# Cross-attention scores: two 64-row tiles of TensorE for four 32-row tiles, with a rest of 16 rows per head

## The chip, the cores and the metric

The kernel runs on one core of a Trainium2 chip. The metric is the device time of one launch in microseconds, as the median of several runs. A profiled execution of the same program gives the trace that the prediction reads. Names of engines: PE is TensorE's matmul, PEld its weight load, DVE VectorE, ACT ScalarE, POOL GpSimd, SP SyncE.

## The reference

There are 16 sequences in a batch, with 100 queries of 640 features, 8 heads of 80 features, and 718 context keys of 384 features (the last 4 of 722 context rows feed a second, small attention). Everything is float32.

```python
query = hidden_states @ Wq            # 100 x 640
keyt = enc @ Wk                       # 718 x 640
valt = enc @ Wv
hs = _mha(query, keyt, valt)          # scores, softmax, weighted values for 8 heads of 80
...                                   # a second attention of x with itself and with 4 tokens: ca_hs2
out = (hs + ca_hs2) @ Wout + b_out + residual
```

What the change touches is the first product in `_mha`: for each sequence, head and key, the dot product of 80 features of the query with 80 features of the key.

## The kernel before

**Tiling.** A loop over the 16 sequences (`for b in range(B)`) does for each of them: scores, the maximum over keys (DVE), the second attention (POOL above all), the next sequence's keys and values (`kk`, `vv`, lines L471 and L440), exponentials (ACT), the weighted values (`a_ps`, L1317), and on some turns the queries of the next two sequences (L541) and the output projection (L951). Inside the loop the order of instructions on every engine is the order in which the Python code issues them (`tc.manual_schedule`); ahead of the loop a scheduler orders them.

**Scores.** Keys lie transposed, `kT[partition, c, u, key]`, in five chunks `c` of 128 partitions; queries likewise in `qp` (chunks 0 to 3, one sequence of 100 columns at a time) and `qz` (chunk 4). The 718 keys are split into six blocks of 119 or 120. A call `scores(b, g, tiles)` makes the scores of two of these blocks (`a` = 0, 1) for all eight heads, so there are three calls for a sequence, one behind the other. Its output has keys on partitions (120) and queries of two heads, 200 columns, side by side in each of four PSUM banks `s_ps[r]`. A head has 80 features: 64 of them lie in chunks 0 to 3 and 16 in chunk 4.

Before the change TensorE is used as four row tiles of 32 rows. Row tile `r` holds the heads 2r and 2r+1: chunk 0 and 1 are the two 32-row halves of the first head's 64 features, chunks 2 and 3 those of the second head, and chunk 4 has 16 rows of each of the two heads. For chunk 4 the queries are in `qz` twice, once masked to the first head's 16 rows and once to the second head's, so one matmul with 200 moving columns serves both heads. The loop order is: block `a`, chunk `c`, row tile `r`. Each matmul names its own stationary 120 key columns. An f32 matmul appears in the trace as two weight loads and two matmul records (two passes).

**Banks.** Calls 0 and 2 take two double banks of pool `ps2`, call 1 takes two banks of `psk` and two of `ps1`. ACT copies finished banks to SBUF (L631, L637). Behind the third call TensorE turns to `now.softmax2()` (L808, output in column tiles of 32) and `second.products()` (L746, the whole array).

**Set-up.** The layout of the features comes from `load_packed`, which loads `Wk` transposed into the chunks by nine DMAs (L305), and from the copies of `Wq` on DVE (L1070 and L1077). Both run once, ahead of the loop.

The functions that the diff touches, with the lines of the profile:

Of the kernel before, what the change touches and what calls it, by code (L numbers as in the profile page):

```python
# [14 lines left out]
B, S, H = 16, 100, 640  # L15
NH, D = 8, 80
CAD, T = 384, 4
SK = 722 - T
P = 128
HC = H // P  # L20
# [3 lines left out]
KN = KT // 2  # L24
# [26 lines left out]
for h in range(NH):  # L51
    lo = h * D
    while lo < (h + 1) * D:
        c = lo // P
        hi = min((h + 1) * D, (c + 1) * P)
        PIECES.append((h, c, lo - h * D, lo - c * P, hi - lo))
        lo = hi
# [15 lines left out]
RG = 4  # L73


def load_packed(load, to, w):

    rows = w.rearrange("(r u k) n -> r u k n", r=RG, u=2)
    for r, u in [(r, u) for r in range(RG) for u in range(2)]:
        load(  # L80
            out=to[32 * r : 32 * r + 32, 2 * u : 2 * u + 2],
            in_=rows[r, u, :64].rearrange("(j p) n -> p j n", j=2),
        )
    load(out=to[:, 4], in_=w.rearrange("(h k) n -> h k n", h=NH)[:, 64:])


# [46 lines left out]
def kernel(  # L133
# [18 lines left out]
    nc = tc.nc  # L152
# [14 lines left out]
    def pair(name):  # L167
        tile = ps2.tile([P, 2, 512], F32, tag="ps2", name=name)
        return tile
# [21 lines left out]
    def scores_tile(name):  # L191
        return main.tile([P, 2, ROWS], F32, tag="st", name=name, bufs=NP)
# [13 lines left out]
    def vb_tile(name):  # L206
        return main.tile([P, T, H], F32, tag="vb", name=name)
# [16 lines left out]
    def load_enc(b):  # L224
        enc = enc_tile(f"enc_{b}"), None
        for u, lo, hi in ((0, 0, 3), (1, 1, 3), (2, 0, 2)):
            at = A_RAW[u, lo]
            nc.sync.dma_start(
                out=enc[0][:, at : at + hi - lo],
                in_=enct[b][:, lo:hi, u * (KT - 1) : u * (KT - 1) + KT],  # L230
            )
        return enc

    def load_rest(b, enc):
        if b == 1:
            room = hsT_tile("rest_1").rearrange("p c s -> p (c s)")
            rest = room[:, : len(A_REST) * KT].rearrange("p (i k) -> p i k", k=KT)
        else:
            rest = rest_tile(f"rest_{b}")
        for (u, c), i in A_REST.items():  # L240
            nc.sync.dma_start(
                out=rest[:, i], in_=enct[b][:, c, u * (KT - 1) : u * (KT - 1) + KT]
            )
        return enc[0], rest
# [6 lines left out]
    def a_form(enc, f):  # L251
        return enc[0][:, A_AT[f]]
# [8 lines left out]
    wq_sb = const.tile([P, HC, H], F32, name="wq_sb")  # L261
    kT = const.tile([P, HC, 3, KT], F32, name="kT")
# [20 lines left out]
    for g in range(2):  # L283
        for c in range(CC):
            nc.scalar.dma_start(
                out=wv_sb[:, 2 * c + g],
                in_=wv[c * P : (c + 1) * P, g * (H // 2) : (g + 1) * (H // 2)],
# [14 lines left out]
    ca_0 = small.tile([S, T, S], F32, tag="ca", name="ca_0", bufs=2)  # L302
    in_order(nc.sync.dma_start(out=ca_0, in_=cas[0].unsqueeze(0).to_broadcast([S, T, S])))
    load_packed(
        lambda **ends: in_order(nc.sync.dma_start(**ends)), wkt_sb[:, :, :CAD], wkt  # L305
    )
    halves = [t[:, u] for t in [scores_tile(f"wq_{i}") for i in range(NP)] for u in range(2)]
    room = halves.pop()
    wq_in = [t[:, :H] for t in halves]
# [19 lines left out]
    for h, c, r, s, k in PIECES:  # L329
        nc.gpsimd.dma_start(  # L330
            out=m2[s : s + k, c, GROUPS[c][1].index(-1), h * T : (h + 1) * T],
            in_=wqcat[h * D + r : h * D + r + k, :],
# [4 lines left out]
    for c in range(HC):  # L337
        first = c * P - HEADS[c][0] * D
        nc.gpsimd.affine_select(
            out=hmask[:, c], in_=hmask[:, c], compare_op=ALU.is_ge, fill=0.0,  # L340
# [3 lines left out]
            out=hmask[:, c], in_=hmask[:, c], compare_op=ALU.is_ge, fill=0.0,  # L344
# [71 lines left out]
    class Values(Blocks):  # L416
# [17 lines left out]
        def product(self, at, f, first, last):  # L434
            for bank in "AB":
                if self.opened[bank] is at and bank in self.fresh:
                    first = True
                    self.fresh.discard(bank)
            for j in range(2):
                nc.tensor.matmul(  # L440
                    at[0][j][:KN, : H // 2],
                    a_form(self.enc, f)[:, j * KN : (j + 1) * KN],
                    wv_there.get(f, wv_sb[:, W_AT[f]]),
                    start=first,
                    stop=last,
                    skip_group_check=True,
                )
# [152 lines left out]
    def scores(b, g, tiles):  # L600

        qp, qz = tiles
        name = f"s_ps_{b}_{g}"
        if g == 1:
            s_ps = [f(f"{name}_{r}") for r, f in enumerate((psumk, psumk, psum1, psum1))]
        else:
            pairs = [pair(f"{name}_{i}") for i in range(2)]
            s_ps = [pairs[r // 2][:, r % 2] for r in range(RG)]
        n = KN
        for a in range(2):  # L610
            u, j = KC[2 * g + a]
            for c in range(HC):
                for r in range(RG):
                    rows = slice(32 * r, 32 * r + 32)
                    if c < 4:
                        rhs = qp[rows, c // 2, c % 2, (b % 2) * S : (b % 2 + 1) * S]
                        lo, hi = (c // 2) * S, (c // 2 + 1) * S
                    else:
                        rhs, lo, hi = qz[rows, 0, b % 2], 0, 2 * S
                    nc.tensor.matmul(  # L620
                        s_ps[r][:n, 256 * a + lo : 256 * a + hi],
                        kT[rows, c, u, j * KN : (j + 1) * KN],
                        rhs,
                        start=(a == 0 and c == 0),
                        stop=(c == HC - 1),
                        skip_group_check=True,
                    )
        st = scores_tile(f"st_{b}_{g}")[:n]
        if g == 1:
            for r in range(RG):  # L630
                nc.scalar.copy(  # L631
                    st[:, :, 2 * r * S : 2 * (r + 1) * S],
                    s_ps[r][:n].rearrange("p (a q) -> p a q", a=2)[:, :, : 2 * S],
                )
        else:
            for i in range(2):
                nc.scalar.copy(  # L637
                    st[:, :, 4 * i * S : 4 * (i + 1) * S].rearrange(
                        "p a (r q) -> p r a q", r=2
                    ),  # L640
                    pairs[i][:n].rearrange("p r (a q) -> p r a q", a=2)[:, :, :, : 2 * S],
                )
        return st
# [81 lines left out]
    class Second:  # L725
# [98 lines left out]
        def load(self):  # L824
            b = self.b
            self.vb = vb = vb_tile(f"vb_{b}")
            nc.gpsimd.dma_start(
                out=vb[:S],
                in_=va_d[b * T : (b + 1) * T, :].unsqueeze(0).to_broadcast([S, T, H]),
            )  # L830
# [179 lines left out]
    for n in range(HC):  # L1010
        for c in range(CC):
            for lo in (0, 64):
# [4 lines left out]
                    start=(c == 0),  # L1017
                    stop=(c == CC - 1),
# [14 lines left out]
    for c in range(HC):  # L1033
        m_ps = psum(f"m_ps_{c}")
        for n, heads in enumerate(HEADS):
# [4 lines left out]
                start=(n == 0),  # L1040
                stop=(n == HC - 1),
                skip_group_check=True,
# [23 lines left out]

    with tc.issue_after(summed.ins):
        for c in range(HC):
            for u in range(2):
                nc.vector.tensor_copy(  # L1070
                    wq_sb[:, c, 2 * u * P : 2 * (u + 1) * P].rearrange(
                        "p (a r k) -> p a r k", a=2, r=RG
                    ),
                    wq_in[c].rearrange("p (r k) -> p r k", r=RG)[:, :, u * D : u * D + 64]
                    .rearrange("p r (a k) -> p a r k", a=2),
                )
            nc.vector.tensor_copy(  # L1077
                wq_sb[:, c, 4 * P :].rearrange("p (h k) -> p h k", h=NH),
                wq_in[c].rearrange("p (h k) -> p h k", h=NH)[:, :, 64:],
            )  # L1080
# [7 lines left out]
    for c in range(CC):  # L1088
        for n in range(2):
# [4 lines left out]
                start=(c == 0),  # L1094
                stop=(c == CC - 1),
# [3 lines left out]
    for n in range(2):  # L1099
        nc.scalar.dma_start(  # L1100
            out=va_d[:, n * (H // 2) : (n + 1) * (H // 2)],
            in_=va[n * B * T : (n + 1) * B * T],
# [10 lines left out]
    last, enc_next, second_next = None, load_rest(1, load_enc(1)), Second(1, xT)  # L1113
# [8 lines left out]
    for b in range(B):  # L1122
        p = b // 2
# [37 lines left out]
        if b == 0:  # L1161
            enc_sums(enc)
            now.load()
            now.softmax1()
        st.append(scores(b, 0, tiles))
        if b == 0:
            now.exponentials1()
        nc.vector.tensor_tensor(most[:KN], st[0][:, 0], st[0][:, 1], ALU.max)
        st.append(scores(b, 1, tiles))
        larger(1)  # L1170
        st.append(scores(b, 2, tiles))

        now.softmax2()
# [131 lines left out]
        for g in range(2):  # L1305
# [6 lines left out]
            for h, i in order:  # L1312
# [3 lines left out]
                for lo, hi in QC:  # L1316
# [4 lines left out]
                        start=(i == 0 and h in (0, *range(4, NH))),  # L1321
                        stop=(i == len(KC) - 1),
                        skip_group_check=True,
# [16 lines left out]
        last = mine  # L1340
# [55 lines left out]
```

## Time and profile before

| | |
|---|---|
| Time, median of 3 runs | 943.8 us (943.6 to 943.82) |
| Span of the profiled execution | 942.4 us, 1.4 us less than the median of the runs |
| PE busy | 934.5 us (99% of the span) |
| PEld busy | 796.2 us (84%) |
| DVE / ACT / POOL busy | 674.0 / 364.7 / 623.1 us |
| Granted TensorE clock | 1.000 over the span |
| `s_ps` matmuls (L620) on the chain that ended last | 12% of the span |

How to read it: the span runs from the first to the last instruction of the profiled execution. Busy time is the union of an engine's records. The duration of a matmul record contains the time that it waits in the array for its weights and a fixed tail, so it is longer than the distance between the starts of consecutive matmuls; rates are read from those distances. Single starts and durations that are named in the prediction and that no shown line contains are those of the same trace, one record at a time.

### The profile page before, as it was taken

The numbers are of one execution on the slowest core, as the hardware profiler recorded it, in microseconds if no ns is written. First come the engines' busy times: TensorE is split into PE (matmuls) and PEld (weight loads), VectorE is DVE, ScalarE is ACT, GpSimd is POOL, SyncE is SP. The second block draws the span as 40 slices with busy tenths as digits, with TensorE's granted clock in tenths as the row PEclk, the third lists the DMA queues.
The fourth block names the chain that finished last, engine by engine and source line by source line (L and its number), as shares of the span: only waits on it lengthen the run. The fifth ranks groups of instructions, "written<-read, shape, count | busy, mean of one in ns | idle before, by whom it ended". The sixth has DMA issues, their size and how long they took to land.

```text
span 942.4 us, 25629 instructions
## 1 busy us (share of the span) xinstructions
PE 934.5 (99%) x11215; PEld 796.2 (84%) x11215; DVE 674.0 (72%) x1084; ACT 364.7 (39%) x605; POOL 623.1 (66%) x565
## 2 busy tenths in 40 slices
PE   9999999999999999999999999999999999999998
PEld 6998979888797888989789887987989888897866
DVE  3559794977929688595955959578693886949684
ACT  1244443524334244433424334244431534334241
POOL 5857976776738757495873948657694576748514
PEclk9999999999999999999999999999999999999999
DMA  8822024040310404003050130403113030210300
GB/s 264 296 60 87 3 70 128 1 130 3 94 60 1 117 2 135 5 11 122 1 151 3 37 82 1 139 1 95 38 40 113 1 112 7 59 53 1 95 8 29
DMA packets 45367, 62.48 MB, mean 66 GB/s; under 512 B 13448, under 2 KB 37320, under 8 KB 43656
## 3 DMA queue, kind: packets, MB, share of 16 engines
q1 hardware_dynamic: 41720, 42.97, 15.2%
q0 software_dynamic: 2512, 16.72, 6.1%
q8 instruction: 88, 1.44, 0.6%
q10 hardware_dynamic: 1024, 1.15, 0.4%
q14 instruction: 23, 0.19, 0.1%
HBM read 55.26 MB, written 5.57 MB: 65 GB/s over the span
## 4 chain that ended last, share of the span: by engine, by line
PE 96%; DVE 3%; issue 0%; DMA 0%; ACT 0%; POOL 0%; ACTq 0%; DVEq 0%
PE s_ps L620 12%; PE a_ps L1317 12%; PE v_psA L440 10%; PE v_psB L440 8%; PE kT_ps L565 8%; PE k_psA L471 7%; PE q_ps L541 7%; PE o_ps L951 7%; PE k_psB L471 6%; PE v_psC L440 3%; PE k_psC L471 3%; PE y_ps L746 2%; PE v_ps L381 2%; PE v_psD L440 2%; PE v_psE L440 2%; PE k_psE L471 1%
## 5 line engine op out<-in xcount | busy, mean ns | idle before, releaser
L781 POOL TENSOR_TENSOR e<-ca,g 100x800 f32<-100x800 f32 x64 | 99.8, 1570 | 145.2 <-DVE most L1156 125.0
L870 POOL TENSOR_TENSOR hs<-vb,p 100x640 f32<-100x640 f32 x64 | 105.6, 1659 | 45.9 <-DVE p L856 32.5
L877 POOL TENSOR_TENSOR hs<-hs,hs 100x640 f32<-100x640 f32 x48 | 113.9, 2373 | 3.8
L1317 PEld LDWEIGHTS a_ps<-vs,st 120*36 120x36 f32 (+3 forms) x3072 | 109.1, 125 | 5.6 <-issue 5.5
L1317 PE MATMUL a_ps<-vs,st 120*36 120x81 f32 (+3 forms) x3072 | 111.9, 233 | 0.0
L440 PE MATMUL v_psA<-wv_sb,enc 128*120 128x320 f32 x352 | 109.5, 434 | 0.0
L506 POOL TENSOR_TENSOR enc<-enc 128x240 f32<-128x240 f32 x135 | 98.1, 736 | 16.9 <-DMA enc<-in_enct 9.8
L1144 DVE TENSOR_TENSOR st<-st,over 120x1600 f32<-120x1600 f32 x48 | 107.6, 2243 | 0.0
L637 ACT COPY st<-s_ps 120x800 f32<-120x800 f32 x64 | 49.7, 829 | 135.6 <-PE s_ps L620 135.6
L620 PE MATMUL s_ps<-qp,kT 32*120 32x100 f32 x3072 | 97.4, 263 | 0.0
L620 PEld LDWEIGHTS s_ps<-qp,kT 32*120 32x120 f32 x3072 | 94.7, 179 | 1.6 <-issue 0.2
L788 POOL TENSOR_TENSOR e<-e,e 100x800 f32<-100x800 f32 x48 | 90.4, 1884 | 3.8
L440 PE MATMUL v_psB<-wv_sb,enc 128*120 128x320 f32 x296 | 91.9, 433 | 0.0
L471 PE MATMUL k_psA<-enc,wk_sb 128*128 128x240 f32 x360 | 87.6, 366 | 0.0
L1329 DVE RECIPROCAL rs<-a_ps 100x4 f32<-100x4 f32 x32 | 5.8, 182 | 111.0 <-PE a_ps L1317 111.0
L1156 DVE TENSOR_TENSOR most<-most,st 120x800 f32<-120x800 f32 x64 | 66.2, 1034 | 24.1 <-ACT st L631 23.0
L1152 ACT ACTIVATE st<-st 120x1600 f32<-120x1600 f32 x48 | 73.9, 1539 | 22.3 <-DVE st L1144 22.2
L471 PEld LDWEIGHTS k_psA<-enc,wk_sb 128*128 128x128 f32 x360 | 68.2, 190 | 16.8 <-DVE kT L411 0.2
L440 PEld LDWEIGHTS v_psA<-wv_sb,enc 128*120 128x120 f32 x352 | 63.2, 183 | 22.6 <-issue 0.5
L471 PE MATMUL k_psB<-enc,wk_sb 128*128 128x240 f32 x300 | 73.1, 366 | 0.3 <-DVE sm L853 0.3
L440 PEld LDWEIGHTS v_psB<-wv_sb,enc 128*120 128x120 f32 x296 | 54.0, 183 | 21.9 <-DVE vs L411 0.4
L541 PE MATMUL q_ps<-xT,wq_sb 128*128 128x200 f32 x400 | 69.1, 333 | 0.0
(146 smaller groups left out, 1732.8 us busy)
## 6 DMA issues: line engine op xcount, KB each, us to landing
vb<-va_d POOLq DMA_DIRECT2D x16, 1000.0 KB, 7.4
enc<-in_enct SPq DMA_DIRECT2D x30, 240.0 KB, 3.9
enc<-in_enct SPq DMA_DIRECT2D x15, 360.0 KB, 3.6
xT<-in_xt SPq DMA_DIRECT2D x8, 500.0 KB, 4.3
rest<-in_enct SPq DMA_DIRECT2D x31, 120.0 KB, 6.6
xn<-in_x SPq DMA_DIRECT2D x11, 320.0 KB, 5.7
out<-xn SPq DMA_DIRECT2D x11, 320.0 KB, 3.2
ca<-in_cas SPq DMA_DIRECT2D x16, 156.2 KB
```

The source lines that it names most:

```text
L440: nc.tensor.matmul(at[0][j][:KN, : H // 2], a_form(self.enc, f)[:, j * KN : (j + 1) * KN], wv_there.get(f, wv_sb[:, W_AT[f]]), start=first ...
L471: nc.tensor.matmul(at[:, i * KT : (i + 1) * KT], wk_sb[:, W_AT[f], i], a_form(self.enc, f), start=(first and i == 0), stop=last, skip_grou ...
L506: nc.gpsimd.tensor_tensor(out, left, right, op)
L541: nc.tensor.matmul(q_ps[:, : 2 * S].rearrange("p (j s) -> p j s", j=2), wq_sb[:, c, n * P : (n + 1) * P], xT[:, :, c, :], start=(c == 0), ...
L565: nc.tensor.matmul(bank[:, i * KT : (i + 1) * KT], weights[c], a_raw(enc, u, c), start=(i == 0 and c == 0), stop=(c == CC - 1), skip_group ...
L620: nc.tensor.matmul(s_ps[r][:n, 256 * a + lo : 256 * a + hi], kT[rows, c, u, j * KN : (j + 1) * KN], rhs, start=(a == 0 and c == 0), stop=( ...
L781: first = nc.gpsimd.tensor_tensor(to, self.ca[:, t, :].unsqueeze(1).to_broadcast([S, NH, S]), g[:, :, t].unsqueeze(2).to_broadcast([S, NH, ...
L788: nc.gpsimd.tensor_tensor(e, e, to, ALU.add)
L870: first = nc.gpsimd.tensor_tensor(to, vb[:S, t, :].rearrange("p (h d) -> p h d", h=NH), p2[:, :, t].unsqueeze(2).to_broadcast([S, NH, D]), ...
L877: nc.gpsimd.tensor_tensor(sums, sums, to, ALU.add)
L1144: return nc.vector.tensor_tensor(st[i], st[i], top.over[:KN].unsqueeze(1).to_broadcast([KN, 2, ROWS]), ALU.subtract,)
L1317: nc.tensor.matmul(a_v[lo:hi, h % 4], st[i // 2][: KEYS[i], i % 2, h * S + lo : h * S + hi], block(i, h // 4)[: KEYS[i], h % 4], start=(i ...
```

## The change

The 64 leading features of a head are contracted in one 64-row tile of TensorE where two 32-row passes were accumulated. Chunk `c` of 0 to 3 now holds the head `c` on partitions 0 to 63 and the head `4 + c` on partitions 64 to 127, so two matmuls of 64 rows and 100 columns stand for four of 32 rows. The rest of 16 rows per head stays as it was: four matmuls of 32 rows with the masked `qz` and 200 columns. In a call all 64-row matmuls of both blocks now stand together, and so do all 32-row matmuls; calls 0 and 2 begin with the 64-row kind, call 1 with the 32-row kind. Weight set-up follows the new layout: eight DMAs of 64 partitions for eight of 32 partitions with the same bytes, and five wide DVE copies for ten. TensorE has 3622 instruction rows in its program for 3878; no other instruction of it moves, and the order on the other engines is the same.

```diff
 def load_packed(load, to, w):
-    rows = w.rearrange("(r u k) n -> r u k n", r=RG, u=2)
-    for r, u in [(r, u) for r in range(RG) for u in range(2)]:
-        load(
-            out=to[32 * r : 32 * r + 32, 2 * u : 2 * u + 2],
-            in_=rows[r, u, :64].rearrange("(j p) n -> p j n", j=2),
-        )
+    rows = w.rearrange("(h k) n -> h k n", h=NH)
+    for half in range(2):
+        for c in range(4):
+            load(
+                out=to[64 * half : 64 * half + 64, c],
+                in_=rows[4 * half + c, :64],
+            )
     load(out=to[:, 4], in_=w.rearrange("(h k) n -> h k n", h=NH)[:, 64:])
...
         n = KN
-        for a in range(2):
+        opened = set()
+
+        def product(a, c, rows, bank, lo, rhs, last):
             u, j = KC[2 * g + a]
-            for c in range(HC):
+            nc.tensor.matmul(
+                s_ps[bank][:n, 256 * a + lo : 256 * a + lo + rhs.shape[-1]],
+                kT[rows, c, u, j * KN : (j + 1) * KN],
+                rhs,
+                start=bank not in opened,
+                stop=last,
+                skip_group_check=True,
+            )
+            opened.add(bank)
+
+        def halves(last):
+            for a in range(2):
+                for c in range(HC - 1):
+                    for half in range(2):
+                        rows = slice(64 * half, 64 * half + 64)
+                        rhs = qp[rows, c // 2, c % 2, (b % 2) * S : (b % 2 + 1) * S]
+                        product(a, c, rows, 2 * half + c // 2, c % 2 * S, rhs, last)
+
+        def rests(last):
+            for a in range(2):
                 for r in range(RG):
                     rows = slice(32 * r, 32 * r + 32)
-                    if c < 4:
-                        rhs = qp[rows, c // 2, c % 2, (b % 2) * S : (b % 2 + 1) * S]
-                        lo, hi = (c // 2) * S, (c // 2 + 1) * S
-                    else:
-                        rhs, lo, hi = qz[rows, 0, b % 2], 0, 2 * S
-                    nc.tensor.matmul(
-                        s_ps[r][:n, 256 * a + lo : 256 * a + hi],
-                        kT[rows, c, u, j * KN : (j + 1) * KN],
-                        rhs,
-                        start=(a == 0 and c == 0),
-                        stop=(c == HC - 1),
-                        skip_group_check=True,
-                    )
+                    product(a, HC - 1, rows, r, 0, qz[rows, 0, b % 2], last)
+
+        for part, last in zip((rests, halves) if g == 1 else (halves, rests), (False, True)):
+            part(last)
...
-            for u in range(2):
-                nc.vector.tensor_copy(
-                    wq_sb[:, c, 2 * u * P : 2 * (u + 1) * P].rearrange(
-                        "p (a r k) -> p a r k", a=2, r=RG
-                    ),
-                    wq_in[c].rearrange("p (r k) -> p r k", r=RG)[:, :, u * D : u * D + 64]
-                    .rearrange("p r (a k) -> p a r k", a=2),
-                )
+            nc.vector.tensor_copy(
+                wq_sb[:, c, : 4 * P].rearrange("p (n i k) -> p i n k", n=4, i=2),
+                wq_in[c].rearrange("p (i n k) -> p i n k", i=2, n=4)[:, :, :, :64],
+            )
```

## The prediction

> **What bounds the kernel.** First the page: how busy each engine is, then the chain of work that ended last.
>
> ```profile
> PE 934.5 (99%) x11215; PEld 796.2 (84%) x11215; DVE 674.0 (72%) x1084; ACT 364.7 (39%) x605; POOL 623.1 (66%) x565
> PEclk9999999999999999999999999999999999999999
> PE 96%; DVE 3%; issue 0%; DMA 0%; ACT 0%; POOL 0%; ACTq 0%; DVEq 0%
> ```
>
> TensorE is the bound, at full clock. Its list of waits holds 1.2 us on DVE in the loop and next to nothing else. So each nanosecond that TensorE needs more or less in the scores reaches the end; nothing is there to absorb it or to take its place.
>
> Next, the timeline of TensorE over one sequence's scores (start us, length us, group, count):
>
> ```profile
> 273.32 0.53 PE L1317 MATMUL a_ps<-vs,st 119*36 119x81 f32 x10
> 273.78 1.10 PE L620 MATMUL s_ps<-qp,kT 32*120 32x100 f32 x32
> 274.69 0.54 PE L620 MATMUL s_ps<-qz,kT 32*120 32x200 f32 x8
> 275.05 1.00 PE L620 MATMUL s_ps<-qp,kT 32*120 32x100 f32 x32
> 275.87 0.54 PE L620 MATMUL s_ps<-qz,kT 32*120 32x200 f32 x8
> ...
> 280.59 0.54 PE L620 MATMUL s_ps<-qz,kT 32*120 32x200 f32 x8
> 281.05 0.75 PE L808 MATMUL z_ps<-y,e 100*32 100x33 f32 x64
> ```
>
> The scores take 281.05 - 273.78 = 7.27 us per sequence, 116 us in all. A block of keys is 32 records of 100 columns (8 rounds: 4 chunks x 2 passes, four tiles side by side) in 0.82 us, then 2 rounds of 200 columns in 0.36 us.
>
> Third, the durations by line (min/median/max ns), which show what a round waits for:
>
> ```profile
> L620 PE MATMUL s_ps<-qp,kT x3072: 244/263/342, 59.8 to 898.6; 32*120 32x100 f32 x192
> L620 PE MATMUL s_ps<-qz,kT x768: 327/338/413, 60.7 to 898.9; 32*120 32x200 f32 x192
> L746 PE MATMUL y_ps<-m,xT x160: 244/260/327, 27.6 to 847.0; 128*100 128x96 f32 x96, 128*100 128x128 f32 x64
> L541 PE MATMUL q_ps<-xT,wq_sb x400: 332/332/437, 51.1 to 830.9; 128*128 128x200 f32 x134
> ```
>
> The 100-column matmul has three durations. 244 (5 rounds per sequence) is the pure one: its weights were loaded under the 200-column round ahead of it, and the next round starts 86 ns later. 263 (42 rounds) is 19 longer: it waits for weights, and rounds are 105 ns apart. 342 (1 round, the first behind `a_ps`) waits 98: its load began only when the tile shape had changed. The 200-column rounds last 347 and 327 by turns, waits of 20 and 0, starts 188 and 169 apart.
>
> **Why 105.** Distances between loads that a next load holds up, read one by one: 58 ns for `k2_ps` (64 columns, two column tiles), 88 for `y_ps` (100 columns, all 128 rows), 112 for `m_ps` (128 columns, all rows), 105 here (120 columns, four 32-row tiles). All four are columns x 0.83 + 5 ns. Neither the number of rows nor the number of tiles enters. One row stands outside: the f32 transposes load 128 columns every 85 ns, but their load records last 142 ns for 190 and the change has none.
>
> **What the change removes.** Half of the 100-column matmuls: 1536 records of 3072. But the rounds stay: 4 chunks x 2 passes per block, now two tiles of 64 rows side by side for four of 32. Each streams 100 columns (86) and loads 120 (105). Two tiles fewer per round start 6.6 ns apart, which the 105 hides. No row has 64-row tiles; from both sides: 32 rows give 105 and 128 rows lie on the same line, so I take 105. If the load were free, the floor is 86.
>
> The Trainium skill prices side-by-side tiles otherwise ("TensorE: Matmul & The Clock Gate", section "The mechanism", and "Measured speedup vs the span model"): the span is one matmul plus about 4 ns for each further tile. By that, two tiles fewer save 8 ns in 48 x 16 rounds, an estimate of 6 us, and the sum below would be 946 us. The trace has no such term where a load bounds the round, so it is not used.
>
> **What it adds: changes of tile shape.** Before, the three calls of a sequence are 32-row work from first to last. After, the order is 64 | 32, 32 | 64, 64 | 32: three more changes per sequence. What a change costs, in two terms:
> - A gap. Distance from the last start of one shape to the first of the next, less the undisturbed distance: 162 - 70 from `a_ps` to `s_ps` (above: last start 273.32 + 0.53 - 0.23 = 273.62, next 273.78), 262 - 169 from `q_ps` to `a_ps`, 362 - 269 from `o_ps` to `a_ps`, 179 - 86 from the transposes to `a_ps`, 257 - 169 from `s_ps` to `z_ps`. That is 88 to 93 whatever the two shapes; I take 93.
> - Weights that are not loaded ahead: 98 here, 437 - 332 = 105 for `q_ps`, 327 - 246 = 81 for `y_ps`: again the load of one tile.
>
> No row has a change between two row heights. The Trainium skill ("TensorEngine Tiling (Array Packing)", "Key Properties") says that a change of tiling mode, not of the tile alone, drains the engine, and lists 64-row and 32-row tiling as different modes; no run here shows that pair, and the sum needs only the rows above. Bounds: zero (32-row tiles inside the 64-row ones need no change) and 93 + 98. Every pair seen costs the upper, so I take it.
>
> **The sum per sequence**, in ns. Streams are the same on both sides: 48 x 86 + 12 x 169 = 6156, and the exit to `z_ps` costs 88 on both.
> - Before: waits 98 + 42 x 19 + 6 x 20 = 1016. Total 6156 + 1016 + 88 = 7260, against 7270 measured.
> - After, 48 rounds of 64 rows: two are first behind a change (98 each), 46 wait 19: 1070. The old rounds without a wait are gone, since no 200-column round stands ahead of them. 12 rounds of 32 rows: two first ones at 98, the others hide their load (105) under the stream (169): 196. Gaps 3 x 93 = 279. Total 6156 + 1070 + 196 + 279 + 88 = 7789.
>
> That is +529 per sequence, +8.5 us over 16. On the profiled execution 942.4 + 8.5 = 950.9; on the median of the runs, which is 1.4 above that span, 952.3.
>
> **Other edits, all at nothing.** The DVE copies (L1070, ten of 284 ns) end at 32.5 us and the queries need them at 51.2; without that cover, five wider copies in place of ten still cost no more. The eight DMAs of `load_packed` carry the same bytes and rows, and stand at the same place of SP's queue (issued from 11.8 to 23.5 us, the `Wq` loads behind them); `w_ps` needs the first of them at 28.2 us, then for chunk 0 the fifth in place of the seventh, and up to 29.1 us the chain waits for POOL's `m2` anyway, so some 0.9 us of cover; without it a late one would cost its lateness once. In call 1 banks 0 and 2 finish some rounds earlier, so ACT's copy may start earlier; it is no bound (39%). In calls 0 and 2 the banks finish together at the end as before, and ACT's two copies of 829 ns fit under the next call's 2.4 us. In the first sequence `qz` comes 66 ns late for its first round (a record of 413); it is needed later now. TensorE's first matmul of call 1 waits for banks that `a_ps` had, as before. All that stands behind the scores moves by the same amount, so no new wait.
>
> **The rivals.**
> - *Half price.* The gap of 93 is paid, but weights are prefetched across a change of row height: waits become 98 + 46 x 19 + 2 x 20 = 1012, +275 per sequence, +4.4 us, 948.2. Against it: every first round behind a change in this trace waits. For it: none of those is between two row heights.
> - *No change of shape.* 32-row and 64-row tiles follow each other like tiles of one kind: 1012 for 1016, 943.7, no change. Against it: five other pairs all pay.
> - *Faster: tiles share the load port.* If 105 were four loads taking turns at 26 ns, two would hide under the stream and 64-row rounds would be 86 apart. Then waits are 2 x 98 + 196 = 392, with gaps 671 for 1016: -345 per sequence, -5.5 us, 938.3. It decides as soon as a 64-row round waits less than 19 - 529/46 = 7.5 ns, that is comes every 93 or less. Against it: one tile of 100 columns takes 88, two of 64 take 58; four in turn would not lie on that line.
> - *Much slower.* Two 64-row loads do not overlap each other: a round of 210, +105 x 46 x 16 = +77 us. Against it: two and four tiles overlap here, with starts 6.6 ns apart.
>
> **How the numbers follow.** Full price 0.68 (952.3), half price 0.14 (948.2), no change of shape 0.09, shared port 0.05, loads in turn 0.04. A measurement here tells about 0.2% (1.9 us) from no change, so slower is 0.68 + 0.14 + 0.04 = 0.86, the same 0.09, faster 0.05. The range takes the first two cases with some room: 946.0 to 955.5.
>
> **What the profile after would show.** 64-row matmuls, 1536 records, most of 263 ns with rounds 105 apart, 64 records of about 342. 32-row matmuls of 200 columns mostly 327, 128 of about 425. A sequence's scores 7.8 us long, and `s_ps` at 13% of the chain. I am wrong if 64-row rounds come under 93 ns apart, if the start behind a change of row height is under 150 ns (100 columns) or 220 ns (200 columns) later, or if the first round behind it does not last longer.

## The result: 951.83 us for 943.81, and the profile after

The changed kernel takes 951.83 us (median of 4 runs, 951.51 to 951.97) beside 943.81 us for the kernel before in the same comparison: a ratio of 1.0084, 95% interval 1.007 to 1.0098. It is slower by 8.0 us. The forecast was 952.3 us, with a range of 946.0 to 955.5. The profiled execution has a span of 950.1 us, 7.7 more than before.

The page after, on the engines and the chain:

```profile
PE 943.5 (99%) x9679; PEld 798.3 (84%) x9679; DVE 681.0 (72%) x1079; ACT 364.6 (38%) x605; POOL 620.7 (65%) x565
PE 96%; DVE 2%; DMA 1%; issue 0%; ACT 0%; POOL 0%; ACTq 0%; DVEq 0%
```

TensorE has 1536 matmul records fewer (768 matmuls of two records each) and is 9.0 us longer busy. It still carries 96% of the chain.

The timeline of TensorE over the scores of the same sequence as before (start us, length us, group, count):

```profile
274.27 0.60 PE L1326 MATMUL a_ps<-vs,st 119*36 119x81 f32 x12
274.80 1.93 PE L615 MATMUL s_ps<-qp,kT 64*120 64x100 f32 x32
276.65 1.63 PE L615 MATMUL s_ps<-qz,kT 32*120 32x200 f32 x32
278.21 3.60 PE L615 MATMUL s_ps<-qp,kT 64*120 64x100 f32 x64
281.75 0.95 PE L615 MATMUL s_ps<-qz,kT 32*120 32x200 f32 x16
282.63 0.75 PE L821 MATMUL z_ps<-y,e 100*32 100x33 f32 x64
```

From 274.80 to the next stage at 282.63 it is 7.83 us for 7.28 before (7276 ns by the single starts). 64 records of the 64-row kind are 32 rounds of two, and they take 281.75 - 278.21 = 3.54 us with the change behind them. Before, 32 rounds of four in the steady 105 ns would have taken 3.36. The single starts are 184, then 30 times 105, then 201 ns apart.

The durations by line (min/median/max ns):

```profile
L615 PE MATMUL s_ps<-qp,kT x1536: 265/265/343, 60.1 to 905.7; 64*120 64x100 f32 x192
L615 PE MATMUL s_ps<-qz,kT x768: 327/328/425, 61.9 to 906.6; 32*120 32x200 f32 x192
```

The 64-row matmul has no short form any more. It lasts 265, or 343 as the first behind a change of shape. The 200-column matmul is 327 or 328 where its load is hidden, and 425 as the first behind a change.

### The profile page after: what moved, and what is told of

Read it like the earlier page. It is cut to its first block, busy times and chain, and to the rows that moved or that the text cites. A ratio compares the mean times of both kernels' runs of the same rounds, so it can differ in the third digit from the quotient of the medians.

```text
span 950.1 us, 22551 instructions
## 1 busy us (share of the span) xinstructions
PE 943.5 (99%) x9679; PEld 798.3 (84%) x9679; DVE 681.0 (72%) x1079; ACT 364.6 (38%) x605; POOL 620.7 (65%) x565
## 4 chain that ended last, share of the span: by engine, by line
PE 96%; DVE 2%; DMA 1%; issue 0%; ACT 0%; POOL 0%; ACTq 0%; DVEq 0%
PE s_ps L615 13%; PE a_ps L1326 12%; PE v_psA L441 10%; PE v_psB L441 8%; PE kT_ps L566 8%; PE k_psA L472 7%; PE q_ps L542 7%; PE o_ps L964 7%; PE k_psB L472 6%; PE v_psC L441 3%; PE k_psC L472 3%; PE v_ps L382 2%; PE y_ps L759 2%; PE v_psD L441 2%; PE v_psE L441 2%; PE k_psE L472 1%
## 5 line engine op out<-in xcount | busy, mean ns | idle before, releaser
L615 PE MATMUL s_ps<-qp,kT 64*120 64x100 f32 x1536 | 88.5, 268 | 0.0
L615 PEld LDWEIGHTS s_ps<-qp,kT 64*120 64x120 f32 x1536 | 83.1, 182 | 5.6 <-issue 4.2
L1165 DVE TENSOR_TENSOR most<-most,st 120x800 f32<-120x800 f32 x64 | 65.9, 1029 | 20.5 <-ACT st L644 19.1
```

Source lines behind the costliest of these rows:

```text
L615: nc.tensor.matmul(s_ps[bank][:n, 256 * a + lo : 256 * a + lo + rhs.shape[-1]], kT[rows, c, u, j * KN : (j + 1) * KN], rhs, start=bank not ...
```

## The experiments

Theory: a round of side-by-side tiles waits for the load of one tile's columns, however many tiles and rows there are, so leaving out half of the instructions brings nothing; and each of the three new changes of row height costs a gap and an unhidden load. The rivals are that the new grouping is to blame, that the price is not one per change, and that rounds wait for something other than the load. Each kernel was compared with the kernel before on the same chip.

**1. The new order with 32-row tiles alone.** The loops of the kernel before, regrouped:

```diff
-        for a in range(2):
-            for c in range(HC):
-                for r in range(RG):
+        quarters, rests = range(HC - 1), range(HC - 1, HC)
+        for part, last in zip((rests, quarters) if g == 1 else (quarters, rests), (False, True)):
+            for a in range(2):
+                for c in part:
+                    for r in range(RG):
```

> The kernel before with the new order alone: all 32-row matmuls of chunks 0 to 3 of both blocks together, those of chunk 4 together, by turns as in the changed kernel, but every tile has 32 rows, so no change of row height within a sequence. Theory (the loss is the three changes of row height): waits 98 + 46 x 19 + 2 x 20 = 1012 ns per sequence for 1016 before, so 943.7 us, within 0.2% of before. Rival (the loss comes from the grouping: chunk-4 rounds standing together no longer cover the loads of the others, or banks finish later): most of the 8 us, 948 to 952.

Measured: 944.37 us for 944.28, ratio 1.0004 (0.9995 to 1.0013). The timeline of the same sequence:

```profile
274.02 1.94 PE L620 MATMUL s_ps<-qp,kT 32*120 32x100 f32 x64
275.78 1.55 PE L620 MATMUL s_ps<-qz,kT 32*120 32x200 f32 x32
277.15 3.52 PE L620 MATMUL s_ps<-qp,kT 32*120 32x100 f32 x128
280.50 0.87 PE L620 MATMUL s_ps<-qz,kT 32*120 32x200 f32 x16
281.30 0.29 PE L818 MATMUL z_ps<-y,e 100*32 100x33 f32 x11
```

(The window ends within the last group.) These are the same groups as in the changed kernel, with twice the 100-column records. From the first to the second group it is 1.76 us here and 1.85 with 64-row tiles, from the second to the third 1.37 and 1.56: the difference stands at the borders. The scores of a sequence take 7276 ns, exactly as before. The grouping costs nothing; the rival falls.

**2. Five and eleven changes in place of three.** For eleven, both functions take the blocks as one more argument.

```diff
-        for part, last in zip((rests, halves) if g == 1 else (halves, rests), (False, True)):
+        for part, last in zip((rests, halves), (False, True)):          # five
...
+        for a in range(2):                                              # eleven
+            halves(False, [a])
+            rests(True, [a])
```

> The changed kernel without the turns: every call does the 32-row matmuls first and the 64-row ones behind, so five changes of row height per sequence for three. Theory (each change costs its gap and an unhidden load): one more first round of each kind (98 - 19 and 98 ns), two more gaps of 108, some 12 less at the exit: +381 ns per sequence, +6.1 us, 957.9. Rival (the price sits in the mixed use as such or in one place, not in each change): 951 to 953.

> The changed kernel with both kinds block by block (64-row, 32-row, 64-row, 32-row in each call): eleven changes per sequence for three. Theory: first rounds 6 + 6 at 98 ns, gaps 6 x 96 + 5 x 108: +1524 ns per sequence, +24.4 us, 976.2. If a change cost the gap alone (load prefetched): +816 ns per sequence, 964.9. Rival (not per change): under 955.

Measured: 959.76 us with five (ratio 1.0165, 1.0151 to 1.0179) and 976.29 us with eleven (1.034, 1.0324 to 1.0356). The timeline with eleven:

```profile
281.08 1.08 PE L615 MATMUL s_ps<-qp,kT 64*120 64x100 f32 x16
282.09 0.61 PE L615 MATMUL s_ps<-qz,kT 32*120 32x200 f32 x8
282.64 1.08 PE L615 MATMUL s_ps<-qp,kT 64*120 64x100 f32 x16
283.65 0.61 PE L615 MATMUL s_ps<-qz,kT 32*120 32x200 f32 x8
```

A block is 1.56 us here for 1.18 in the kernel before. The scores of a sequence take 7276, 7831, 8212 and 9355 ns with no, three, five and eleven changes. The last two are +381 and +1524 on the changed kernel, which are the expected numbers to the nanosecond: some 185 to 191 ns for each change. The expectation had its prices (96, 108 and 98 ns) from the trace of the changed kernel; what these runs show is that the same prices come again at each further change. With five the whole is 1.9 us above the forecast of 957.9. The scores explain 6.1 us as expected. The rest is two waits: the first call now begins with `qz` and waits 0.8 us for ACT's copy, and a wait on DVE in the second sequence is 1.6 us for 0.6 in the changed kernel:

```profile
PE k_psE L472 <- DVE vs L412: 1.6, 1, 1.6
PE s_ps L615 <- ACT qz L554: 0.8, 1, 0.8
```

The price is one per change, gap and unhidden load both.

**3. Fewer stationary columns, with four tiles and with two.** Chunks 0 to 3 with 100 key columns for 120 (they leave out those features for 20 keys of each block); in the four-tile kernel chunk 4 stands first:

```diff
+            keys = 100 if c < HC - 1 else n
             nc.tensor.matmul(
-                s_ps[bank][:n, 256 * a + lo : 256 * a + lo + rhs.shape[-1]],
-                kT[rows, c, u, j * KN : (j + 1) * KN],
+                s_ps[bank][:keys, 256 * a + lo : 256 * a + lo + rhs.shape[-1]],
+                kT[rows, c, u, j * KN : j * KN + keys],
```

> The kernel before (four 32-row tiles) with the stationary of chunks 0 to 3 cut from 120 to 100 key columns; chunk 4 keeps 120 and stands first in each block. It leaves out chunks 0 to 3 of 20 keys in each block. Moving columns, tiles and rounds are the same. Theory (a round waits for a load of columns x 0.83 + 5 ns): rounds come 88 apart for 105, 42 x 17 + 20 ns less per sequence, -11.7 us, 932.1. Rival (the 19 ns are the start-up of three further tiles, 6.6 ns each, or the stream): rounds stay at 105, 943.5.

> The version with five changes of row height, with the stationary of the 64-row matmuls cut from 120 to 100 key columns (it leaves out 64 features of 20 keys in each block). Theory (the load of 64-row tiles costs by columns like that of 32-row tiles): 64-row rounds 88 apart for 105 and the first of each group 17 shorter, 48 x 17 = 816 ns per sequence, 13.1 us less than the version with 120 columns. Rival (64-row rounds are bound by something else): no change.

Measured: 936.7 us with four tiles (ratio 0.9921, 0.9907 to 0.9934). With two tiles and five changes 946.3 us (1.0021, 1.0012 to 1.0031), for 959.76 with 120 columns: 13.5 us less where 13.1 were expected (the scores give 12.8 of it). The durations of the 100-column matmul, first with four tiles, then with two:

```profile
L621 PE MATMUL s_ps<-qp,kT x3072: 241/247/325, 61.5 to 891.1; 32*100 32x100 f32 x192
```

```profile
L616 PE MATMUL s_ps<-qp,kT x1536: 248/248/327, 61.4 to 900.8; 64*100 64x100 f32 x192
```

The common duration falls from 263 to 247 and from 265 to 248, and steady rounds are 88 to 89 ns apart in both. The moving columns and the tiles are as before; only the load is shorter. So the load bounds the round, alike for 32 and 64 rows, and the rival of the three further tiles falls.

With four tiles the whole fell by 7.6 us, 4 less than expected, though the scores lost 11.3 (116.48 to 105.23 us). About 1.2 us of the rest are at the start (`qz` comes late for the first round again, 0.8). The others are pauses behind the scores that were not there before:

```profile
PE z_ps L809 <- issue: 1.7, 4, 0.6
PE s_ps L621 <- ACT qz L553: 0.8, 1, 0.8
```

In four sequences TensorE stops in the middle of `z_ps` and the profile names no releaser. The trace points at TensorE's own instructions: each of the four stops begins 1.8 to 2.2 us behind the start of a 16-KB transfer on the instruction queue q8, which has only 88 of them in the run, one per 10.6 us. (They are 76 in the changed kernel, whose TensorE has 3072 records of loads and matmuls fewer: 256 for each transfer.) The regrouped kernel of experiment 1 has three such stops in `z_ps`, 2.2 to 2.5 us behind such a transfer, 0.7 us together, though its scores are no shorter. That late instructions cause the stops is not tested.

**4. Fewer moving columns with two tiles.** 80 query columns for 100 (the last 20 queries of each head lose 64 features), five changes:

```diff
-                        rhs = qp[rows, c // 2, c % 2, (b % 2) * S : (b % 2 + 1) * S]
+                        rhs = qp[rows, c // 2, c % 2, (b % 2) * S : (b % 2) * S + 80]
```

> The version with five changes of row height, with the 64-row matmuls streaming 80 query columns in place of 100 (it leaves out 64 features for the last 20 queries of each head). Theory (a round waits for its load of 120 columns): rounds stay 105 apart, the wait inside a record grows; only the last round of a group ends 17 ns earlier: about 0.7 us less. Rival (the stream binds): 17 ns less in each of 48 rounds, 13 us less.

Measured: 958.95 us, 0.8 less than with 100 columns. The duration of the 64-row matmul:

```profile
L615 PE MATMUL s_ps<-qp,kT x1536: 265/265/327, 62.2 to 914.1; 64*120 64x80 f32 x192
```

A fifth less of stream buys nothing inside a group: the rounds stay 105 ns apart, and a sequence gains 50 ns, 17 at the end of each of its three groups. This is the counterpart of the shorter load.

**5. The rounds alone.** Without chunk 4 (16 of each head's 80 features left out) neither kernel has a change of row height in the scores:

```diff
-        for part, last in zip((rests, halves) if g == 1 else (halves, rests), (False, True)):
-            part(last)
+        halves(True)                                # two 64-row tiles
...
-            for c in range(HC):
+            for c in range(HC - 1):                 # four 32-row tiles
```

> The changed kernel without chunk 4 (it leaves out 16 of each head's 80 features): only the 48 rounds of two 64-row tiles, no change of row height. Theory: 48 x 86 + 98 + 47 x 19 + exit 100 = 5.2 us per sequence for 7.3 before, about 911 us (to 914 if ACT's copies bind), and the same as the next kernel within 0.1%. Rival (fewer tiles per round are cheaper, 6.6 ns for each tile): 10 us less than the next kernel.

> The kernel before without chunk 4 (it leaves out 16 of each head's 80 features): 48 rounds of four 32-row tiles. Theory: the same rounds of 105 ns as with two 64-row tiles, about 911 us (to 914 if ACT's copies bind). Rival: slower than the two-tile version by up to 10 us.

Measured: 917.44 us with two tiles (ratio 0.9715, 0.9701 to 0.973) and 919.71 us with four (0.9737, 0.9723 to 0.9752). The timeline of one sequence's scores, first with two tiles, with the copies of ACT that the next paragraph needs, then with four:

```profile
268.83 5.54 PE L615 MATMUL s_ps<-qp,kT 64*120 64x100 f32 x96
...
270.84 1.55 ACT L649 COPY st<-s_ps 120x800 f32<-120x800 f32 x2 [7.31 <-PE s_ps L615]
```

```profile
269.98 5.55 PE L620 MATMUL s_ps<-qp,kT 32*120 32x100 f32 x192
```

The scores of a sequence take 5465 and 5485 ns, and steady rounds are 105 ns apart in both, so the tiles themselves make 0.3 us over the whole. Most of the other 2 us is at the start: in the profiled run with four tiles `k2_ps` begins at 20.5 us for 18.7 with two. It begins at 18.4 in the kernel before, whose tiles and set-up are those of the four-tile kernel, so this part does not come from the tiles.

Both are above the 911 us that were expected, by 6.4 and 8.7 us, and above the 914 too. With two tiles, 3.9 us of it are in the scores (5465 ns for 5219), in part because ACT's copies bind. ACT has copied the last banks of the first call at 270.84 + 1.55 = 272.39. The third call needs these banks for its second row tile. Its first row tile starts on time, at 272.27, but the second starts at 272.45, 53 ns behind the copy, and its record lasts 343 ns, the length of an unhidden load. Another 2.0 us are behind the scores of the first two sequences, where TensorE pauses longer than in the kernel before.

No kernel here beats the one before: the regrouped one equals it, and the three shorter times leave work out.

## Why the prediction was right

The forecast was a sum of steps, and nearly all of them stand:
- **Rounds.** Two 64-row tiles come every 105 ns, as taken from the 32-row and 128-row loads. Experiments 3 and 4 show the reason: the load sets the distance, the stream does not, and the number of tiles does not.
- **Loss of the cover.** 46 of 48 rounds wait for their load, where five of 48 did not before. The 200-column rounds standing together lose that wait in return; experiment 1 shows that the two cancel.
- **Unhidden loads.** Taken as 98. The first two rounds behind a change start 184 ns apart with 100 columns and 267 with 200, which is 98 above the undisturbed 86 and 169; the first records last 343 and 425.
- **Gaps.** Taken as 93 for each change. From 64 rows to 32 rows the first starts of the rounds are 201 apart, 96 above the steady 105. From 32 to 64 rows they are 277 apart, 108 above 169. Here the term was mis-sized by 15 ns: the exit row (257) was read from the last of four tiles, which starts 20 ns after the first, and the undisturbed distance from the first. Read in that way, the new pairs give 195 - 105 = 90 and 257 - 169 = 88, like the other rows; but a sum over first starts has to add the 20 ns of four tiles, or the 6 of two. With the other 6 ns of the gaps and some rounding the scores grew by 556 ns per sequence for 529.
- **What the whole made of it.** 16 x 556 = 8.9 us in the scores, but 7.7 in the span and 8.0 in the time. Here the prediction was wrong in a small thing: it said that nothing would absorb the loss, though the list of waits in the loop held 1.8 us in three entries, and it named only the 1.2. In the first two sequences TensorE's waits on DVE took up 1.3 us: the stretches behind their scores are 0.77 and 0.55 us shorter. Before:

```profile
PE k_psE L471 <- DVE vs L411: 1.2, 1, 1.2
PE k_psB L471 <- DVE sm L853: 0.3, 1, 0.3
PE k_psC L471 <- DVE kT L411: 0.3, 1, 0.3
```

After, of these three:

```profile
PE k_psE L472 <- DVE vs L412: 0.6, 1, 0.6
```

DVE reached these points as early as before, and TensorE came later: `k_psC` and `k_psE` start behind their waits at 86.13 and 122.04 us before, at 86.14 and 122.05 after. The two small misses, 0.4 us of gaps and 1.3 us absorbed, have opposite signs, and a start 0.3 us later in the profiled run takes back part of the second. That the forecast of 952.3 us came within 0.5 us is partly luck, then; the mechanism is not.

- **Other edits.** Taken as nothing. The later start lies ahead of `k2_ps` (18.67 us for 18.39); from there to the first scores it is 41.40 us in both kernels, so the new set-up cost nothing.
- **The rivals.** Half price and no change of shape fell by the gaps and the first records of the trace after, and by experiment 2. The shared load port fell by 105 with two tiles: four loads in turn would have left two hidden. Loads in turn fell by the same number.
- **The two rules of the Trainium skill that were weighed.** By the span model of "TensorE: Matmul & The Clock Gate" (section "Measured speedup vs the span model") each tile less would save about 4 ns in every round; 5465 and 5485 ns for 48 rounds in experiment 5 leave 0.4 ns per round for two tiles less, so it does not price rounds that a load bounds. "TensorEngine Tiling (Array Packing)" lists 64-row and 32-row tiling as different modes ("Available Configurations") and says that a change of mode drains the engine ("Key Properties"). The trace after agrees in so far as each change costs a gap of 96 or 108 ns.

## What to carry to other kernels

Before trading several small tiles for fewer large ones, look at what a round of side-by-side tiles waits for. In this kernel a matmul's record was longer than its pure form (263 for 244 ns) because of the load of one tile's stationary columns. Fewer columns per load shortened the round, and under a longer stream (the 200-column rounds) the load was hidden; half as many instructions, or a shorter stream, did not help. Count the changes of tile shape that a layout brings, and price each with the gap and the unhidden load that the trace already shows for other pairs of shapes, both distances of a gap read from the same tile of a round. Where two kinds of tile have to be mixed, put equal kinds side by side, since each border cost some 190 ns here.

## What the runs showed of the hardware that was not expected

Tiles of different row height in the same array, both with the full width of columns, pay the same price for a change as tiles of quite different forms: from the last start of one shape to the first of the next, 90 and 88 ns above the undisturbed distance, beside 88 to 93 for five other pairs. Counted from the first tile of a round it is 96 behind two row tiles and 108 behind four, since the further tiles start 6 to 7 ns after one another. A change also leaves the next load unhidden: 98 ns for 120 columns, and 81 for 100 (the first two rounds start 167 apart in the two-tile kernel with 100 stationary columns, 86 of it stream). The recorded duration of a matmul does not follow its stream where the load binds: with 80 moving columns it stayed at 265 ns, as with 100.
